# Another order for the same work: a planner that shakes its due times by a stored list of seeds

## The chip, the cores and the metric

The kernel runs on one core of one Trainium2 chip. Five engines matter here: TensorE (PE), VectorE (DVE), ScalarE (ACT), GpSimd (POOL) and SyncE (SP). Each runs its own instructions in the order in which they stand in the program, and waits on semaphores for the others. SP and POOL issue nearly all the DMA transfers of this kernel. The metric is device microseconds (us), the median over runs; lower is better.

## The reference

The input `x` has two batches of 1024 rows by 2048. Each batch goes through a quantized product with its own context matrix and then through a feed-forward product with one shared matrix of ternary weights. Both are added to the row they came from, with a gate:

```python
def fake_quant(x, scale, zp):
    q = jnp.clip(jnp.round(x / s + z), 0.0, 255.0)
    return (q - z) * s
...
# feed-forward
s = 127.0 / jnp.clip(jnp.max(jnp.abs(x), axis=-1, keepdims=True), 1e-05, None)
xq = jnp.clip(jnp.round(x * s), -128.0, 127.0) / s
scale_w = 1.0 / jnp.clip(jnp.mean(jnp.abs(weight)), 1e-5, None)
tw = jnp.clip(jnp.round(weight * scale_w), -1.0, 1.0)
out = jnp.einsum('bsi,oi->bso', xq, tw) / scale_w
...
x = x + jnp.tanh(g_xattn[0]) * matmul(fake_quant(layernorm(x)), fake_quant(ctx))
x = x + jnp.tanh(g_ffn[0]) * feed_forward(layernorm(x), weight)
```

## The kernel before

A batch is eight row tiles of 128 rows; tiles 0 to 7 are batch 0, tiles 8 to 15 are batch 1, and the two share eight places in `resid`. The kernel has these kinds of work, each of them written as a function that hands steps to a planner:

- `norm1` takes the statistics of a row tile (four instructions of 512 columns on DVE, then the aggregate), the root on ACT, a chain of small DVE instructions, the quantizer on ACT, eight transposes on PE (`turn_steps`), and two copies of the transposed tile from PSUM into the arena, each on ACT or on DVE.
- `context` loads 1 MB of the context (a chunk: 256 rows by 1024 columns, so eight chunks for each half `h`), rounds it on ACT (L612) and clips it on DVE (L616).
- `first` is the product of one row tile with one half of the context: eight units of four matmuls (L641), one for each chunk, and one addition to the residual on DVE (L647).
- `norm2`, `weight_load`, `weight_sum`, `weight_scale` and `weight_turn` prepare the second stage. The weights come in twice for nine of the sixteen row tiles: once for the mean of their magnitudes, once to be quantized, turned on PE (L1054) and clipped (L1062, L1064).
- `couple` and `plain` are the second product for batch 0 (matmuls at L778 and L824). For batch 1, `differences` and `bring_back` make sums and differences of weight blocks and `seven` does the product with seven block products where eight would be usual (L949).
- `evict2` adds a finished product to the residual (L762), `store` writes it out (L769).

Three product buffers (`mm`) and two transpose buffers (`tr`) fill the PSUM. The arena in SBUF has 32 slots, for which contexts, weights and turned tiles compete.

The order of all this is not written by hand. Every step has its engine or engines, a modelled duration, a due time, and what it reads, writes, takes and gives back. `Order.run` plays the steps forward once in modelled time. At each turn it takes, over all engines, the step that can start first, and among those that tie to 1e-6 us the one that is due first. `work_back` plays the result backward and gives each step the latest time at which it could have started; these times are the due times of the next run. `give_out(12)` does twelve such rounds, keeps the run with the smallest modelled end, and then calls the steps in that order. Where a step may go to ACT or DVE, `run` sends it to the one that would end it sooner.

The planner's times are only a model. The real order on each engine is what it gives out; the real times come from semaphores. Four loads stand outside of it: the entry function issues the row tiles 0 (in two halves), 1 and 2 itself, before the branch, always in the order of L1997 (issued at L1998). In the plan they are steps on a made-up engine `PRE` that issues nothing (L462).

Of the kernel before, what the change touches and what calls it, by code (L numbers as in the profile page):

```python
# [108 lines left out]
class Order:  # L109
# [5 lines left out]
    START = {"PRE": 0.5}  # L115
    BRANCH = 4.6

# [35 lines left out]
    @staticmethod  # L153
    def room(pool, k, reserve=0, prefer=None):

        ends = sorted(t for t, _ in pool)
        at = ends[k + reserve - 1]
        if k == 2:
            at = max(at, min(max(pool[i][0], pool[i + 1][0]) for i in range(0, len(pool) - 1, 2)))
        return at  # L160

    @staticmethod
    def pick(pool, at, k, reserve=0, prefer=None):
        if k == 2:
            for i in prefer or range(0, len(pool) - 1, 2):
                if max(pool[i][0], pool[i + 1][0]) <= at + 1e-9:
                    return [i, i + 1]
        if prefer is None:
            return [min(range(len(pool)), key=lambda i: (pool[i][0], i))]
        for i in prefer:  # L170
            if pool[i][0] <= at + 1e-9:
                return [i]

    def run(self, due):
        steps, N = self.steps, len(self.steps)
        waits = [len(s[3]) for s in steps]
        early = [s[7] for s in steps]
        pools = {k: [(0.0, -1)] * n for k, n in self.sizes.items()}
        left = dict(self.users)
        till = {}  # L180
        free, open_ = {}, {}
        dma_free, dma_last = 0.0, -1
        begin, end, where, slots = [0.0] * N, [0.0] * N, [None] * N, [None] * N
        pred = [[] for _ in steps]
        links = self.links = [{} for _ in steps]
        last = {}
        order = []

        def put(n):
            for e, w in steps[n][0]:  # L190
                open_.setdefault(e, {})[n] = w

        for n in range(N):
            if not waits[n]:
                put(n)
        for _ in range(N):
            best = None
            for e, cand in open_.items():
                fe = free.get(e, self.START.get(e, self.BRANCH))
                for n, w in cand.items():  # L200
                    at = early[n]
                    if at < fe:
                        at = fe
                    if best is not None and at > best[0] + 1e-6:
                        continue
                    take = steps[n][4]
                    if take:
                        at = max(at, self.room(pools[take[0]], *take[1:]))
                        if at == float("inf"):
                            continue  # L210
                    if len(steps[n][0]) > 1:
                        key = (at, due[n], n, at + w, e)
                    else:
                        key = (at, due[n], n, 0.0, e)
                    if best is None or at < best[0] - 1e-6 or key[1:] < best[1:]:
                        best = key
            if best is None:
                self.stuck = [n for c in open_.values() for n in c], order, slots
                return None
            at, _, n, _, e = best  # L220
            ways, _, _, _, take, give, dma, _ = steps[n]
            if len(ways) > 1:
                ends = []
                for e2, w2 in ways:
                    ends.append((max(at, free.get(e2, self.BRANCH)) + w2, e2, w2))
                fin, e, w = min(ends)
                at = fin - w
            else:
                w = ways[0][1]
            for e2, _ in ways:  # L230
                del open_[e2][n]
            if take:
                pool = pools[take[0]]
                idx = slots[n] = self.pick(pool, at, *take[1:])
                for i in idx:
                    if pool[i][1] >= 0:
                        pred[n].append(pool[i][1])
                        links[n][pool[i][1]] = True
                    pool[i] = (float("inf"), -1)
            if e in last:  # L240
                pred[n].append(last[e])
            last[e] = n
            begin[n] = at
            where[n] = e
            fin = at + w
            free[e] = fin
            if dma:
                if dma_last >= 0:
                    pred[n].append(~dma_last)
                dma_free = max(dma_free, fin) + abs(dma)  # L250
                dma_last = n
                fin = dma_free + self.LANDING
            end[n] = fin
            order.append(n)
            for m, i in give:
                for j in range(steps[m][4][1]) if i is None else (i,):
                    left[m, j] -= 1
                    t = till.get((m, j))
                    if t is None or fin + self.LAG > t[0]:
                        t = (fin + self.LAG, n)  # L260
                    till[m, j] = t
                    if not left[m, j]:
                        pools[steps[m][4][0]][slots[m][j]] = t
            for m in self.follow[n]:
                same = len(steps[m][0]) == 1 and steps[m][0][0][0] == e and not dma
                t = fin + (0.0 if same else self.LAG)
                if t > early[m]:
                    early[m] = t
                waits[m] -= 1
                if not waits[m]:  # L270
                    put(m)
        return order, begin, end, where, slots, pred
# [45 lines left out]

    def give_out(self, runs=12, tell=None):
        self.prepare()  # L320
        due = [s[1] for s in self.steps]
        best = None
        for r in range(runs):
            res = self.run(due)
            if res is None:
                if tell:
                    tell("stuck")
                break
            if tell:
                tell(f"run {r}: {max(res[2]):.2f}")  # L330
            if best is None or max(res[2]) < max(best[2]):
                best = res
            back = self.work_back(res)
            due = back
        assert best is not None, "the steps that are left wait for each other's buffers"
        self.best = best
        order, begin, end, where, slots, pred = best
        for n in order:
# [6 lines left out]
def centred(  # L345
# [198 lines left out]
    def norm1(tiles, due, pieces=1):  # L544
# [33 lines left out]
        for i, t in enumerate(tiles):  # L578
# [12 lines left out]
            for g in range(pieces):  # L591
                m = step(
                    "ACT", 0.3 + 1.85 / pieces, due, (lambda f, g: lambda slots=None: f(g, slots))(quant, g),
                    rd=[key("sc")] + xk(t), wr=[k2("q", g)], take=None if g else ("q8", 1),
                )
                by = by if g else m
# [32 lines left out]
    def first(t, h, due):  # L629
# [22 lines left out]
        for c in range(C):  # L652
            give = [cx[b, h, c]["by"]]
            if c == C - 1:
                give.append(turned["aT", t, "by"])
            n = step(
                "PE", 0.865, due, (lambda c: lambda slots=None: mult(c, slots))(c),
                rd=[("aT", t, 2 * c // C), ("ca", b, h, c)], wr=[("pm", t)],
# [5 lines left out]
    def norm2(tiles, due):  # L664
# [4 lines left out]
        def mean(i, t):  # L669
            if i == 0:  # L670
                s["nm"], s["vm"] = tiny(n), tiny(2 * n)
# [113 lines left out]

    def couple(ta, tb, q, due, pieces, last):

        s = {}
        by = None
        for n, (o0, o1) in enumerate(pieces):  # L790
            for i, t in enumerate((ta, tb)):
# [5 lines left out]

                w = 16 * (0.027 + 0.0472 * (o1 - o0))
                end = last and n == len(pieces) - 1
                m = step(  # L800
# [9 lines left out]

    def plain(t, h, due, last):
        s = {}
        by = None
        for i in range(2):
# [14 lines left out]
            for c0 in (0, 4):  # L829
                end = last and i == 1 and c0 == 4  # L830
                m = step(
                    "PE", 1.73, due, (lambda f, c0: lambda slots=None: f(c0, slots))(mult, c0),
                    rd=q_keys(t, q, 0, 4), wr=[("pl", t, h)], take=None if (i or c0) else ("mm", 1),
# [66 lines left out]
    def seven(ta, tb, due, final=False):  # L900
# [39 lines left out]
        for k, (name, bank, left, right, need, new, dest) in enumerate(products):  # L940
# [19 lines left out]
            for i, (cs, ns) in enumerate(parts):  # L960
                give = []
                if i == len(parts) - 1:
# [6 lines left out]
                m = step(  # L969
                    "PE", 3.46 / len(parts), due + 3.46 * (k + i / len(parts)),  # L970
                    (lambda f, cs, ns: lambda slots=None: f(cs, ns, slots))(mult, cs, ns),
# [165 lines left out]
    for q in range(NQ):  # L1137
        for ta in (0, 2):
            pieces = [(o, o + 1) for o in range(4)] if q == 0 else [(0, 4)]
            couple(ta, ta + 1, q, due, pieces, q == NQ - 1)  # L1140
            due += 6.9
    for t in range(4, MT):
        for h in range(2):
            plain(t, h, due, h == 1)
            due += 6.9
# [23 lines left out]

    plan.give_out(12)  # L1170

# [867 lines left out]
```

## Time and profile before

| | |
|---|---|
| median of 3 runs | 484.92 us (484.38 to 485.58) |
| the profiled execution | 485.77 us |
| its span, first to last instruction | 484.0 us |
| PE busy | 454.3 us |
| DVE busy | 340.6 us |
| ACT busy | 258.4 us |
| DMA, mean over the span | 211 GB/s |
| first transposes on PE | 12.72 us |
| first product on PE | 21.23 us |

The profile lists instructions by line, engine and operation. A "wait" names the engine and line that came last before an idle engine went on. The granted clock of PE was 0.996 in the mean. Matmuls overlap in the records, so the sum of their durations is larger than the busy time. Up to about 95 us the DMA queues move around 400 GB/s (rows, contexts and weights of batch 0).

### The profile page before, as it was taken

The page shows a single profiled execution, that of the slowest core. Times are in us where ns is not written, and L with a number is a line of the kernel's source. Part 1 is how long each engine was busy: PE and PEld are TensorE (multiplying, and loading weights), DVE is VectorE, ACT ScalarE, POOL GpSimd, SP SyncE. Part 2 cuts the span into 40 slices and gives each one's busy share as a digit, 9 for nine tenths or more (in the row PEclk, how much of TensorE's full clock was granted, in tenths as well). Part 3 has the DMA queues.
Part 4 walks back from the last instruction along what each step waited for, and adds up shares of the span by engine and source line. Part 5 has one row for each costly group of instructions (what it writes and reads, how often), then busy time and mean ns, then how long its engine had stood idle before and what let it go on. Part 6 is the DMA issues. An engine that isn't in the chain of part 4 may idle for free.

```text
span 484.0 us, 6296 instructions
## 1 busy us (share of the span) xinstructions
PE 454.3 (94%) x2564; PEld 225.0 (46%) x2564; DVE 340.6 (70%) x534; ACT 258.4 (53%) x200; POOL 21.2 (4%) x39
## 2 busy tenths in 40 slices
PE   0499999999999999999998999999999999999994
PEld 0244444444588545444444444444444454444442
DVE  4988899928789987798975997124776987333342
ACT  3886699867989998711129663002656770000000
POOL 0000000000031101111101000000000000000000
PEclk9999999999999999999999999999999999999998
DMA  8999999791099986899979411062000012131304
GB/s 318 405 415 413 413 419 389 267 357 78 1 362 393 332 293 185 244 387 393 398 318 335 187 45 43 1 244 105 0 0 1 1 43 108 68 130 45 130 22 158
DMA packets 21857, 102.20 MB, mean 211 GB/s; under 512 B 1980, under 2 KB 1980, under 8 KB 16700
## 3 DMA queue, kind: packets, MB, share of 16 engines
q1 hardware_dynamic: 15008, 67.11, 35.0%
q0 software_dynamic: 6800, 34.61, 20.0%
q8 instruction: 22, 0.36, 0.3%
q14 instruction: 15, 0.12, 0.1%
q10 hardware_dynamic: 12, 0.00, 0.0%
HBM read 80.74 MB, written 20.97 MB: 210 GB/s over the span
## 4 chain that ended last, share of the span: by engine, by line
PE 71%; DMA 11%; ACT 7%; DVE 5%; issue 4%; DVEq 0%; ACTq 0%; POOL 0%; POOLq 0%
PE mm L641 42%; PE mm L949 20%; DMA arena<-in_ctx_dram 9%; PE mm L778 6%; ACT bytes L1047 3%; PE tr L513 3%; ACT bytes L586 2%; DMA out_dram<-resid 2%; DVE arena L521 1%; DVE arena L1064 1%; ACT arena L612 1%; DVE resid L762 1%; DMA row<-in_L_xattn_x_zp_dram 1%; DVE resid L647 1%; DVE strip L685 0%
## 5 line engine op out<-in xcount | busy, mean ns | idle before, releaser
L641 PE MATMUL mm<-arena 128*128 128x512 f16 x1024 | 226.2, 380 | 3.1 <-ACT arena L521 1.9
L641 PEld LDWEIGHTS <-arena 128*128 128x128 f16 x1024 | 99.2, 98 | 119.8 <-ACT arena L521 2.0
L949 PE MATMUL mm<-arena 128*128 128x512 fp8e4 x448 | 97.5, 379 | 0.0
L762 DVE SCALAR_TENSOR_TENSOR resid<-mm,am,resid 128x1024 f32<-128x1024 f32 (+1 forms) x53 | 58.0, 1099 | 55.6 <-PE mm L949 44.6
L612 ACT ACTIVATE arena<-arena,scal 128x2048 int16<-128x2048 f32 x32 | 62.8, 1994 | 42.7 <-DMA arena<-in_ctx_dram 42.7
L647 DVE SCALAR_TENSOR_TENSOR resid<-mm,scal,resid 128x1024 f32<-128x1024 f32 x32 | 40.8, 1281 | 42.9 <-PE mm L641 31.6
L949 PEld LDWEIGHTS <-arena 128*128 128x128 f16 x448 | 43.7, 98 | 51.9
L778 PE MATMUL mm<-arena 128*128 128x128 fp8e4 (+1 forms) x448 | 58.2, 288 | 0.9 <-DVE resid L762 0.9
L824 PE MATMUL mm<-arena 128*128 128x512 fp8e4 x256 | 55.6, 379 | 0.0
L679 ACT ACTIVATE arena<-resid,strip 128x2048 f32<-128x2048 f32 x16 | 32.0, 2000 | 40.7 <-DVE strip L673 40.6
L685 DVE TENSOR_REDUCE strip<-arena 128x1 f32<-128x2048 f32 x16 | 36.5, 2279 | 11.8 <-ACT arena L679 11.8
L521 ACT CAST arena<-tr 128x1024 f16<-128x1024 int8 x37 | 36.1, 1009 | 14.4 <-PE tr L513 12.4
L778 PEld LDWEIGHTS <-arena 128*128 128x128 f16 x448 | 33.2, 98 | 22.5 <-issue 1.0
L550 DVE BATCH_NORM_STATS2 stats<-resid 128x6 f32<-128x512 f32 x64 | 39.8, 674 | 0.8 <-DVE off_centre L2002 0.8
L824 PEld LDWEIGHTS <-arena 128*128 128x128 f16 x256 | 25.0, 98 | 30.0
L586 ACT ACTIVATE bytes<-resid,strip 128x2048 int8<-128x2048 f32 (+1 forms) x17 | 33.2, 1985 | 10.5 <-DVE strip L569 10.5
L521 DVE CAST arena<-tr 128x1024 f16<-128x1024 int8 x27 | 32.7, 1217 | 5.2 <-PE tr L513 4.3
L861 DVE TENSOR_TENSOR arena<-arena 128x2048 fp8e4<-128x2048 fp8e4 x16 | 35.9, 2275 | 0.0
L735 ACT ACTIVATE bytes<-resid,strip 128x2048 int8<-128x2048 f32 x16 | 33.0, 2087 | 3.8 <-DVE strip L708 3.8
L1047 ACT ACTIVATE bytes<-arena,scal 128x2048 int8<-128x2048 f32 x16 | 31.4, 2000 | 0.0
L513 PE MATMUL tr<-ident,bytes 128*128 128x128 f16 x256 | 20.0, 224 | 11.5 <-ACT bytes L586 9.6
L1064 DVE TENSOR_SCALAR arena<-tr 128x1024 fp8e4<-128x1024 int8 x23 | 27.1, 1216 | 3.4 <-PE tr L1054 2.4
(61 smaller groups left out, 185.7 us busy)
## 6 DMA issues: line engine op xcount, KB each, us to landing
arena<-in_ctx_dram SPq DMA_DIRECT2D x16, 1024.0 KB, 13.7
arena<-in_L_ffn_weight_dram SPq DMA_DIRECT2D x16, 1024.0 KB, 8.3
arena<-in_ctx_dram POOLq DMA_DIRECT2D x16, 1024.0 KB, 8.7
out_dram<-resid SPq DMA_DIRECT2D x31, 512.0 KB, 7.0
arena<-in_L_ffn_weight_dram POOLq DMA_DIRECT2D x9, 1024.0 KB, 8.8
resid<-in_x_dram POOLq DMA_DIRECT2D x8, 1024.0 KB, 12.6
resid<-in_x_dram SPq DMA_DIRECT2D x7, 1024.0 KB, 16.0
awayT<-arena SPq DMA_DIRECT2D x8, 512.0 KB, 4.5
```

What stands on the lines that cost most here:

```text
L521: (nc.scalar.copy if engine == "ACT" else nc.vector.tensor_copy)(d[:, ts(h, n)], v[:, ts(h, n)])
L550: nc.vector.bn_stats(stats6[:, t % 4, c, :], res(t)[:, ts(c, 512)])
L586: nc.scalar.activation(q["q"][:, ts(g, w)], res(t)[:, ts(g, w)], AF.Identity, bias=s["bi"][:, i : i + 1], scale=s["sc"][:, i : i + 1],)
L612: nc.scalar.activation(slot16(slots[0]).bitcast(I16), s["w"], AF.Identity, scale=rs2)
L641: nc.tensor.matmul(pm[t][:, ts(q, U)], a[:, c, j, :], o[:, j, ts(q, U)], start=(c + j == 0), stop=(c + j == C),)
L647: nc.vector.scalar_tensor_tensor(v, pm[t], g1, v, ALU.mult, ALU.add, accum_out=acc[:, i : i + 1])
L685: nc.vector.tensor_reduce(s["vm"][:, n + i : n + i + 1], s["dev", t], AX.X, ALU.max)
L762: lambda: nc.vector.scalar_tensor_tensor(v, ps(), am2[:, t : t + 1], v, ALU.mult, ALU.add),
L778: nc.tensor.matmul(ps[:, o0 * P : o1 * P], a[:, c, j, :], w[:, j, o0:o1], start=(c + j == 0), stop=(c + j == C),)
L824: nc.tensor.matmul(s["pm"][:, ts(i, U)], a[:, c, j, :], w[:, j, :], start=(c + j == 0), stop=(c + j == C),)
L949: nc.tensor.matmul(s[bank][:, ts(n, U)], a[:, c, j, :], v[:, c, j], start=new and c + j == 0, stop=c + j == 4, skip_group_check=not new,)
L1047: nc.scalar.activation(s["q"], wl[ot]["w"], AF.Identity, scale=sw)
```

## The change

The planner gets new rules for its choice, and its result is shaken.

- `run` looks at all open steps. Among those that can start no later than 0.3 us (`WIN`) after the earliest, it takes the one that is due first.
- A step with two engines goes where it would end first, after a `lean` of its own is added to its second engine.
- `settle` does the twelve rounds as before. After that, `give_out` goes through 95 stored seeds. Each of them shifts the due times (and the leans) of the steps around one moment by random amounts; the shifts add up. Then `run` plays the steps once with the shaken times, and that order is used.
- The modelled start after the branch moves from 4.6 to 5.4 us, and some modelled PE durations go down by about 1%.
- `couple` and `plain` give back the slot of a turned tile after all of their pieces, where only those of the last columns did so; `norm1` and `norm2` no longer assume which tile of a pair comes first.

No step is added or taken away, and each step does what it did.

```diff
-    BRANCH = 4.6
+    BRANCH = 5.4
+    WIN = 0.3
+    LEAN = 0.0
...
-    def run(self, due):
+    def run(self, due, lean):
...
+            open_ += ready
+            rooms, ways = {}, {}
+            for n in open_:
+                at, take = early[n], steps[n][4]
+                if take:
+                    kind = take[0], take[1], take[2] if len(take) > 2 else 0
+                    if kind not in rooms:
+                        rooms[kind] = self.room(pools[kind[0]], *kind[1:])
+                    at = max(at, rooms[kind])
+                best = None
+                for i, (e, w) in enumerate(steps[n][0]):
+                    s = max(at, free.get(e, self.START.get(e, self.BRANCH)))
+                    f = s + w + (lean[n] if i else 0.0)
+                    if best is None or f < best[0]:
+                        best = f, s, e, w
+                ways[n] = best
+            first = min(b[1] for b in ways.values())
...
+            n = min((due[n], n) for n in open_ if ways[n][1] <= first + self.WIN)[1]
...
+    def shake(self, due, lean, begin, seed):
+        r = random.Random(seed)
+        span = max(begin)
+        mid, half = r.uniform(0.0, span), r.choice((4.0, 12.0, 40.0, span))
+        share, by = r.choice((0.1, 0.3, 1.0)), r.choice((2.0, 6.0, 15.0))
+        due, lean = list(due), list(lean)
+        for n, t in enumerate(begin):
+            if abs(t - mid) <= half and r.random() < share:
+                due[n] += r.gauss(0.0, by)
+                if len(self.steps[n][0]) > 1:
+                    lean[n] += r.gauss(0.0, 0.8)
+        return due, lean
...
+    def give_out(self, seeds=()):
         self.prepare()
...
+        res, due, lean = self.settle()
+        begin = res[1]
+        for seed in seeds:
+            due, lean = self.shake(due, lean, begin, seed)
+        if seeds:
+            res = self.run(due, lean)
...
-                "PE", 0.865, due, (lambda c: lambda slots=None: mult(c, slots))(c),
+                "PE", 0.855, due, (lambda c: lambda slots=None: mult(c, slots))(c),
...
-                end = last and n == len(pieces) - 1
+                end = n == len(pieces) - 1
...
-    plan.give_out(12)
+    plan.give_out((
+        596853, 876363, 279267, 840775, 26681, 303858, 939078, 813524, 764831, 209546, 902833, 961729,
...
+    ))
```

## The prediction

> **What bounds the kernel now.** I read the page's busy shares first, then the slices, then who TensorE (PE) waited for, then the opening in order of time.
>
> ```profile
> span 484.0 us, 6296 instructions
> PE 454.3 (94%) x2564; PEld 225.0 (46%) x2564; DVE 340.6 (70%) x534; ACT 258.4 (53%) x200; POOL 21.2 (4%) x39
> PE   0499999999999999999998999999999999999994
> ```
>
> PE is the bound: 454.3 of 484.0, and its row of slices is full but for the two at the front and the last. The time to be had or lost is PE's idle time, 29.7 us. The view of PE's waits says where it lies:
>
> ```profile
> PE tr L513 <- ACT bytes L586: 9.6, 2, 5.2
> PE tr L444 <- ACT row L2003: 7.7, 1, 7.7
> PE mm L641 <- ACT arena L521: 1.9, 1, 1.9
> PE tr L513 <- DVE arena L521: 1.3, 1, 1.3
> PE mm L778 <- DVE resid L762: 0.9, 1, 0.9
> PE mm L641 <- DVE arena L616: 0.8, 2, 0.6
> ```
>
> 9.6 + 7.7 + 1.3 = 18.6 us are the opening, before PE's first product. The other waits, with three under 0.7 us (0.6, 0.5, 0.3), are 1.9 + 0.9 + 0.8 + 1.4 = 5.0 us in all. The remaining 6.2 us are the tail behind PE's last matmul (477.8 to 484.0). So a new order can win at most 5.0 us behind the opening, unless it shortens the opening or the tail. The opening, in order of time (start, duration, engine):
>
> ```profile
> 5.74 0.69 DVE L550 BATCH_NORM_STATS2 stats<-resid 128x6 f32<-128x512 f32 x1 [0.78 <-DVE off_centre L2002]
> 6.35 1.86 DVE L550 BATCH_NORM_STATS2 stats<-resid 128x6 f32<-128x512 f32 x3
> 8.25 0.26 DVE L555 BATCH_NORM_AGGREGATE strip<-stats 128x2 f32<-128x24 f32 x1
> 8.59 1.28 ACT L559 ACT_TABLE_LOAD   x1 [0.93 <-DVE strip L555]
> ...
> 11.43 2.37 ACT L586 ACTIVATE bytes<-resid,strip 128x1024 int8<-128x1024 f32 x2 [1.25 <-DVE strip L569]
> 12.72 0.61 PE L513 MATMUL tr<-ident,bytes 128*128 128x128 f16 x4 [4.42 <-ACT bytes L586]
> ...
> 20.40 1.03 PE L513 MATMUL tr<-ident,bytes 128*128 128x128 f16 x8 [5.17 <-ACT bytes L586]
> 21.23 3.68 PE L641 MATMUL mm<-arena 128*128 128x512 f16 x12
> ...
> 26.68 3.63 PE L641 MATMUL mm<-arena 128*128 128x512 f16 x16 [0.46 <-DVE arena L521]
> ```
>
> Four statistics of row tile 0, its mean and variance, the root on ScalarE (ACT), the quantizer, the transposes: one serial chain that nothing hides. From 21.23 on PE hardly stops. The loads that the chain stands on (issues, and time to landing):
>
> ```profile
> L1998 SPq DMA_DIRECT2D resid<-in_x_dram x4: 327/360/415, 0.7 to 4.8; - x4
> DMA to landing us min/median/max: 4.1/5.0/6.6
> ```
>
> The first half of tile 0 lands at 0.75 + 4.1 = 4.9, the second (issued 1.24) at 1.24 + 5.0 = 6.2, tile 2 (issued 4.8) at 4.8 + 6.6 = 11.4. Tile 1, as large as tile 2, stands between the last two; half way, 8.8, is my estimate for it.
>
> **The change, part by part.** No instruction is added or taken away on PE: 477 planned steps in both orders, so PE's own work is worth 0. Four clips or copies go over from VectorE (DVE) to ACT; both have idle time, worth 0 on the path as long as neither is what PE waits for. The lower weights (0.855 for 0.865 and so on), the window and the leanings cost nothing themselves; they only choose the order. So I walk the new order, with durations from the rows of before.
>
> *Opening.* In the planner's own list the load of row tile 1 now stands ahead of the second half of tile 0. But these four loads are not issued by the planner: the entry function issues them in a fixed order, tile 0's second half first. On DVE the new order is: two statistics of tile 0, one of tile 1, the two of the scales (L447, L448), and only then the last two of tile 0. Queued behind the statistic that waits for tile 1 are therefore the whole chain above, and ACT and PE behind it. DVE: two statistics to 7.0; tile 1 lands at 8.8, statistic to 9.5; the scales 0.24; two statistics 1.24 to 11.0; so the aggregate starts at 11.05 instead of 8.25, **+2.8**. Bounds: landing at 6.2 would leave 0.7 + 0.24 = +0.9, landing at 11.4 +5.4. I take 8.8, by sizes.
>
> The quantizer starts at 14.25, its halves end at 16.6. ACT's new order: copy of the first transposes 16.65 to 17.65, root of tile 1 to 18.0, two context chunks (1.9 each, where now one stands there) to 21.85, root of tile 2, which waits for DVE's aggregate at 21.95, to 22.3, then tile 1's quantizer, 2.05, to 24.35. PE's order still has tile 1's transposes ahead of the first product, so they start at 24.4 instead of 20.40: **+4.0**, my term for the opening.
>
> *What PE regains to 75 us.* Then the first products find more chunks ready. T1, T2 stand for eight transposes (0.45 us), a unit is four matmuls at 71.66 / 332 = 0.2158 us each (the chain's long stretch), 0.863 us. New order: two units, T2 (its quantizer ends at 26.4), then units for tiles 1, 2 and 0, whose last inputs, DVE's copies at 27.8 and 29.0 and clip at 29.7, come before PE is there. I followed the queues to the transposes of tile 7: every input came ahead of PE, the narrowest by under 1 us (tile 2's second copy, 40.9). The three waits of this stretch now (0.5, 0.2, 0.6) are saved, 1.3. Loads in this stretch come at the rate of the DMA queues (412 GB/s in 21 to 45 us); the SP order differs in the first two chunks alone, worth 0.
>
> Weighed against a rule: the first 12 matmuls took 3.52 us up to the next transposes, 0.29 each, and 16 later ones 0.227 each, while the window around them shows a granted clock of 1.00. The Trainium skill, "TensorE: Matmul & The Clock Gate", Part 1, says that the array runs at half rate until about 3.4 us of sustained work and falls back after an idle window of that length. By it the longer wait (18.3 to 24.4 here) speaks against the change; but the present gap of 5.17 us is over the limit too, so by the rule and by the row the slow start is paid once in each order: 0. If only the new gap paid, up to 1.7 us (estimate from that page) would be added.
>
> *Feed-forward weights, 118 to 205 us.* The waits of 0.9, 0.6 and 0.3 here come from two transpose buffers and three product buffers. The new order puts the sum of the weights behind 104 product units instead of 113 and ends the weight turns later (24 couples and 6 plain pieces ahead of the last one, now 23 and 0), so ACT and DVE have more time per turn: saved 1.8. My walk finds one new wait, at weight tile 6, where both transpose buffers are full until DVE has clipped tile 5: 0.7.
>
> *Turn to batch 1.* Now:
>
> ```profile
> 259.20 2.00 ACT L612 ACTIVATE arena<-arena,scal 128x2048 int16<-128x2048 f32 x1 [0.45 <-DMA arena<-in_ctx_dram]
> 261.11 2.08 ACT L586 ACTIVATE bytes<-resid,strip 128x2048 int8<-128x2048 f32 x1
> 264.14 2.12 PE L641 MATMUL mm<-arena 128*128 128x512 f16 x9 [1.85 <-ACT arena L521]
> ```
>
> A chunk that came late holds ACT, and ACT holds the copy that PE wants: 1.85 us. In the new order three plain pieces (5.2 us) stand between the transposes of tiles 8 and 9 and the first product. Tile 0's last store is now some 14 us of PE work nearer to this place, and POOL loads tile 8 after it: store 7.0, load 12.6 to landing, still ahead of need. Saved 1.85.
>
> *Rest.* From 264 to the last matmul PE idles 0.1 now; the new interleaving of banks can only lose. Bounds: 0, and 5.0, as much as the present order loses. I take 0.8, what PE now loses to late clips (L616). The tail has the same last piece (half a bank, one store of 256 KB) behind a store issued 0.4 us before PE ends, as now: 0, still 6.2.
>
> **Sum.** +4.0 opening, -5.0 (1.3 + 1.8 + 1.9) waits gone, +0.7 + 0.8 new: +0.5. The profiled execution took 485.77 with its span of 484.0 (1.77 around it); that is 0.85 above the median, 484.92, to which I apply the difference: **485.4 us**. A difference below 0.3% (1.45 us) counts as no change, about what a measurement can tell.
>
> **Rivals.**
>
> 1. *The late opening stays* (slower). DVE, ACT and PE are all shifted by the same wait for tile 1, so waits between them return as they were: +4.0, 488.9. For it: in 21 to 45 us DVE is busy 20.2 of 24 us and ACT 19.2, so neither catches up quickly. Against: the chunks loaded meanwhile. It decides once new waits pass 2.5 us.
>
> 2. *Tile 1 lands early, or no new wait comes* (faster). At a landing of 6.2 the aggregate is 0.95 late instead of 2.8: 485.4 - 1.85 = 483.5. Without new waits 485.4 - 1.5 = 483.9, with both 482.0; I price the case at 483.2. Against: tiles 1 and 2 share the 5.2 us between the landings at 6.2 and 11.4, 2.6 us per MB, the 405 GB/s that the page has for the second slice.
>
> 3. *The order hardly changes*: ruled out, PE's sixth step already differs.
>
> **How the numbers follow.** Forecast 0.40, rival 1 0.38, rival 2 0.22. Range: from 483.2 less 0.5 for my reading of the opening, 482.7, to 488.9 plus 0.9 for one more wait like that at L778, 489.8. Faster 0.22, same 0.40, slower 0.38.
>
> **What would show it.** In the changed profile (lines stand 8 earlier): DVE's third statistic starts near 8.8 behind a wait for a load; first transposes near 15.5, tile 1's near 24.4; no wait over 1 us at the first product of batch 1; a tail of 6.2. I am wrong if the third statistic starts by 7.5, if PE waits over 2.5 us in all behind 25 us, or if a store or a load of batch 1 holds it near 260.

## The result, and the profile after

The changed kernel took 488.67 us (median of four runs, 488.02 to 489.27) where the kernel before took 484.73 beside it (four runs, 484.38 to 485.58). The ratio is 1.0079, with a 95% interval of 1.0060 to 1.0097: slower by 0.8%, or 3.9 us. The forecast of 485.4 was 3.3 us too low; the range of 482.7 to 489.8 holds the result. The prediction had given "same" a chance of 0.40 and "slower" 0.38.

The profiled execution took 488.58 us, 2.8 more than that of before (485.77); its span is 486.8, also 2.8 more. The profiled run of before lay 1.0 above its own median and that of after 0.1 below, which is the rest of the 3.9. All sums below are in spans and have to explain 2.8.

The head of the page, the kernel after:

```profile
span 486.8 us, 6291 instructions
PE 455.7 (94%) x2564; PEld 225.8 (46%) x2564; DVE 337.3 (69%) x530; ACT 262.7 (54%) x203; POOL 21.2 (4%) x39
PE   0199999999998999989999999999999999999995
PEclk9999999999999999998999999999999999999999
```

PE has the same 2564 matmuls and transposes, yet is busy 1.4 us longer. Behind the opening its row of slices (12.2 us each) has an 8 in the slices from 146 and from 207 us, and the row of the granted clock has its 8 next to the second, from 219 us on. PE's waits, the kernel after (engine, line, what came last; us in total, times, longest):

```profile
PE tr L505 <- ACT bytes L578: 13.0, 2, 7.4
PE tr L436 <- ACT row L2004: 7.5, 1, 7.5
PE mm L770 <- DVE resid L754: 2.0, 1, 2.0
PE tr L505 <- ACT arena L513: 1.4, 1, 1.4
PE tr L505 <- DVE arena L1056: 1.2, 2, 1.0
```

The opening is 13.0 + 7.5 + 1.4 = 21.9 where it was 18.6: **+3.3**. The other waits are 2.0 + 1.2 = 3.2 where they were 5.0: **-1.8**. All waits of before behind the opening are gone, the batch turn's 1.85 among them; two new places, at 153 to 158 us and at 216 us, took 3.2 back. With **+1.4** of busy time and a tail of 6.0 for 6.2 (**-0.2**) the sum is +2.7, the 2.8 up to rounding.

The opening in order of time, the kernel after (start, duration, engine):

```profile
5.48 1.29 DVE L542 BATCH_NORM_STATS2 stats<-resid 128x6 f32<-128x512 f32 x2
8.94 0.69 DVE L542 BATCH_NORM_STATS2 stats<-resid 128x6 f32<-128x512 f32 x1 [2.18 <-DMA resid<-in_x_dram]
9.55 0.14 DVE L439 COPY scal<-tr 128x4 f32<-128x4 f32 x1
9.69 1.27 DVE L542 BATCH_NORM_STATS2 stats<-resid 128x6 f32<-128x512 f32 x2
10.99 0.26 DVE L547 BATCH_NORM_AGGREGATE strip<-stats 128x2 f32<-128x24 f32 x1
...
15.47 0.61 PE L505 MATMUL tr<-ident,bytes 128*128 128x128 f16 x4 [7.44 <-ACT bytes L578]
...
23.65 1.03 PE L505 MATMUL tr<-ident,bytes 128*128 128x128 f16 x8 [5.57 <-ACT bytes L578]
24.48 3.26 PE L633 MATMUL mm<-arena 128*128 128x512 f16 x8
```

The third statistic is row tile 1's, and it waits 2.18 us for that load. Everything behind it in DVE's queue, the last two statistics of tile 0 above all, is 2.74 us later than before (aggregate 10.99 for 8.25), and so are the quantizer and the first transposes.

Now a stretch that the prediction's walk left out. In order of time, the kernel after, 207 to 226 us:

```profile
207.19 7.07 PE L770 MATMUL mm<-arena 128*128 128x512 fp8e4 x32
214.09 1.89 PE L816 MATMUL mm<-arena 128*128 128x512 fp8e4 x8
214.30 0.75 DVE L754 SCALAR_TENSOR_TENSOR resid<-mm,am,resid 128x512 f32<-128x512 f32 x1 [4.13 <-PE mm L770]
214.97 2.28 DVE L853 TENSOR_TENSOR arena<-arena 128x2048 fp8e4<-128x2048 fp8e4 x1
217.16 0.74 DVE L754 SCALAR_TENSOR_TENSOR resid<-mm,am,resid 128x512 f32<-128x512 f32 x1
217.96 8.32 PE L770 MATMUL mm<-arena 128*128 128x512 fp8e4 x30 [1.98 <-DVE resid L754]
```

PE makes the two products of a couple (32 matmuls) and eight matmuls of a plain piece; then it wants a free product buffer. The couple's two additions free it. DVE idles 4.13 us until the products are ready, does the first addition, then a weight difference of 2.28 us (L853) that stands between the two in its queue, and only then the second. PE waits 1.98 us, and what follows costs as much again. Windows over the same stretch (window, us, busy us of PE, PEld, DVE, ACT and POOL with their counts, granted clock, DMA share, GB/s), the kernel after:

```profile
205.00:216.00 11.00, 10.98 (x51) 4.90 (x50) 6.87 (x6) 5.27 (x4) 0.71 (x1) 1.00 0.51 144
218.40:221.80 3.40, 3.40 (x10) 1.19 (x9) 3.40 (x2) 0.00 (x0) 1.80 (x3) 0.50 0.85 270
221.80:230.00 8.20, 8.20 (x39) 3.72 (x38) 3.75 (x4) 0.94 (x1) 0.70 (x1) 1.00 0.99 380
```

For 3.41 us PE's granted clock is 0.50: 10 matmuls in a stretch that holds some 16 at the rate of the line below (39 in 8.20). Half of 3.41 is 1.7 us, and that is PE's longer busy time, but for -0.3 that I can't place.

### The profile page after: what moved, and what is told of

Read it like the earlier page. It is cut to its first block, busy times and chain, and to the rows that moved or that the text cites. A ratio compares the mean times of both kernels' runs of the same rounds, so it can differ in the third digit from the quotient of the medians.

```text
span 486.8 us, 6291 instructions
## 1 busy us (share of the span) xinstructions
PE 455.7 (94%) x2564; PEld 225.8 (46%) x2564; DVE 337.3 (69%) x530; ACT 262.7 (54%) x203; POOL 21.2 (4%) x39
## 4 chain that ended last, share of the span: by engine, by line
PE 90%; ACT 3%; DVE 2%; issue 1%
PE mm L633 45%; PE mm L941 20%; PE mm L816 11%; PE mm L770 10%; PE tr L505 3%; PE tr L1046 1%; DVE arena L1056 1%; ACT bytes L578 1%; ACT bytes L1039 1%; ACT arena L604 1%; ACT arena L513 1%; DVE arena L853 0%; DVE resid L754 0%; DVE arena L513 0%; ACT arena L1054 0%
## 5 line engine op out<-in xcount | busy, mean ns | idle before, releaser
L770 PE MATMUL mm<-arena 128*128 128x128 fp8e4 (+1 forms) x448 | 60.2, 292 | 2.0 <-DVE resid L754 2.0
L513 ACT CAST arena<-tr 128x1024 f16<-128x1024 int8 x41 | 39.9, 1012 | 25.5 <-PE tr L505 20.4
L853 DVE TENSOR_TENSOR arena<-arena 128x2048 fp8e4<-128x2048 fp8e4 x16 | 36.1, 2280 | 0.0
L513 DVE CAST arena<-tr 128x1024 f16<-128x1024 int8 x23 | 27.7, 1217 | 7.0 <-PE tr L505 6.9
L1056 DVE TENSOR_SCALAR arena<-tr 128x1024 fp8e4<-128x1024 int8 x22 | 26.0, 1218 | 7.1 <-ACT arena L1054 5.4
```

What stands on the lines that cost most here:

```text
L513: (nc.scalar.copy if engine == "ACT" else nc.vector.tensor_copy)(d[:, ts(h, n)], v[:, ts(h, n)])
L770: nc.tensor.matmul(ps[:, o0 * P : o1 * P], a[:, c, j, :], w[:, j, o0:o1], start=(c + j == 0), stop=(c + j == C),)
```

## The experiments

Theory, after the comparison: the loss has two separate parts, each one step given out at a bad place. (A) Tile 1's statistic and the scales ahead of tile 0's last statistics, some 2.5 to 3 us. (B) One weight difference between two additions at 214 us, 2 us of waiting and 1.7 us of half clock. The rival: the new order shifts everything, these two are only where it shows, and with either mended the loss turns up elsewhere. Seven of the kernels move one, two or three steps after the plan is made; nothing else changes. Step 20 is the first statistic of row tile 1, steps 5 to 8 are the four of tile 0, step 1 the scales, steps 11 and 12 small DVE steps of tile 0 behind the aggregate; 516 and 517 are the two products of the couple at 207 us, 518 and 520 their additions, 935 the weight difference.

**Tile 1's statistic behind tile 0's four**

```
         self.best = order, begin, end, where, slots, pred = res
+        order = list(order)
+        order.remove(20)
+        order.insert(order.index(8) + 1, 20)
```

> The changed kernel with one step moved: on VectorE the first statistic of row tile 1 stands behind the four of tile 0, not ahead of the last two. Theory A (the opening's wait for tile 1 is paid at the end): the wait of 2.2 us at the third statistic goes, first transposes near 12.5 instead of 15.5, those of tile 1 near 21 instead of 23.7, and 488.7 falls by 2 to 3 us to about 486. Rival (context chunks come too late anyway, the wait is hidden): PE idles later for what it gains, and the time stays within 0.7 us of 488.7. The wait of 2.0 us near 216 us and the slow clock after it stay under both.

487.65 us, ratio to the kernel before 1.0057 (1.0038 to 1.0076): 1 us won, not 2 to 3. A miss, and the opening of this kernel shows why:

```profile
8.09 0.16 DVE L442 COPY scal<-tr 128x4 f32<-128x4 f32 x1 [1.30 <-PE tr L439]
8.24 1.86 DVE L545 BATCH_NORM_STATS2 stats<-resid 128x6 f32<-128x512 f32 x3
10.02 0.24 DVE L550 BATCH_NORM_AGGREGATE strip<-stats 128x2 f32<-128x24 f32 x1
14.48 0.61 PE L508 MATMUL tr<-ident,bytes 128*128 128x128 f16 x4 [6.43 <-ACT bytes L581]
```

The scales (L442, L443) still stood ahead of tile 0's last two statistics. They need a small product of PE that is ready only at 8.09. Behind tile 1's load that had cost nothing; with that load out of the way it became the wait, 1.30 us, and one statistic of tile 1 still runs ahead of the aggregate. One wait had hidden another.

**The second addition ahead of the weight difference**

```
         self.best = order, begin, end, where, slots, pred = res
+        order = list(order)
+        order.remove(520)
+        order.insert(order.index(935), 520)
```

> The changed kernel with one step moved: on VectorE the residual addition of row tile 1 (last columns of batch 0's couple) stands ahead of the difference T2/0 that now holds it for 2.3 us. Theory B (the wait near 216 us is this queue, and the half clock from 218.4 to 221.8 follows from the wait): both go, 2.0 + 1.7 us, so about 485.0. Rival 1 (the clock falls on its own account): the wait goes, the half clock stays, about 486.7. Rival 2 (PE waits for something else behind it, such as weights or a buffer): no change, 488.7.

484.99 us, ratio 1.0001 (0.9989 to 1.0013), span 483.0: 3.8 us less than the kernel after. The same place, now with both additions together:

```profile
214.12 1.89 PE L819 MATMUL mm<-arena 128*128 128x512 fp8e4 x8
214.32 1.41 DVE L757 SCALAR_TENSOR_TENSOR resid<-mm,am,resid 128x512 f32<-128x512 f32 x2 [4.13 <-PE mm L773]
215.85 7.07 PE L773 MATMUL mm<-arena 128*128 128x512 fp8e4 x32
```

and its window:

```profile
218.40:221.80 3.40, 3.40 (x17) 1.56 (x16) 3.40 (x2) 0.00 (x0) 1.79 (x3) 1.00 0.55 166
```

PE no longer waits, the clock stays at 1.00 and the same window holds 17 matmuls for 10. PE is busy 453.8 us, 1.9 less than in the kernel after. One step moved by one place in DVE's queue takes both the 2.0 and the half clock away. That is part B, and shown.

**Both of these moves**

```
+        order.remove(20)
+        order.insert(order.index(8) + 1, 20)
+        order.remove(520)
+        order.insert(order.index(935), 520)
```

> The changed kernel with both moves of the two runs before. Theory A and B together, if the two are independent: 2.7 + 3.7 us less, about 482.3, which is faster than the kernel before (484.7). If the opening is hidden: 485.0; if the clock falls anyway: 484.0.

484.03 us, ratio 0.9979 (0.9967 to 0.9991). Short of the expectation by 1.7 us, as the first move was by itself: this run had the same half mended opening.

**The kernel before, with tile 1's statistic moved to where the new order has it**

```
         order, begin, end, where, slots, pred = best
+        order = list(order)
+        order.remove(20)
+        order.insert(order.index(7), 20)
```

> The kernel before with the opening's fault alone: on VectorE the first statistic of row tile 1 stands ahead of the last two of tile 0. Theory A: it waits for the load till about 8.9, the chain starts 2.8 us later, less the 0.6 us that this statistic would take later, and nothing behind makes it up: 484.7 + 2 to 3 = 487.2. Rival (the opening has slack, the loss comes from elsewhere): within 0.7 us of 484.7.

488.90 us, ratio 1.0077 (1.0056 to 1.0098), span 486.9, +2.9 against before; I had expected +2 to +3 on the time, and by medians it was more. This one step alone makes the old order as slow as the new one. Its opening:

```profile
8.93 1.88 DVE L553 BATCH_NORM_STATS2 stats<-resid 128x6 f32<-128x512 f32 x3 [2.12 <-DMA resid<-in_x_dram]
23.01 1.04 PE L516 MATMUL tr<-ident,bytes 128*128 128x128 f16 x8 [5.17 <-ACT bytes L589]
23.84 4.85 PE L644 MATMUL mm<-arena 128*128 128x512 f16 x12
```

Tile 1's transposes start 2.6 later (23.01 for 20.40), the first twelve matmuls take 1.2 longer (4.85 for 3.68), and the batch turn's wait shrinks from 1.85 to 1.02: +2.6 + 1.2 - 0.8 = +3.0. The old order's other waits are all still there. Here rival 1's mechanism, everything shifted together, is seen at work.

**The new order with the opening as before**

```
         self.best = order, begin, end, where, slots, pred = res
+        order = list(order)
+        order.remove(1)
+        order.insert(order.index(11) + 1, 1)
+        order.remove(20)
+        order.insert(order.index(12) + 1, 20)
```

> The changed kernel with VectorE's whole opening as in the kernel before: the four statistics of tile 0, their aggregate, then the scales, then the chain, and tile 1 behind it. The run with one step moved still had the scales ahead of tile 0's last statistics, and these wait till about 8.0 us for PE's small product. Theory A: first transposes near 12.5, those of tile 1 near 20.9 (23.7 in the changed kernel), the time 488.7 less 2 to 2.8, about 486.2; the wait near 215 us and a half clock behind it stay. Rival (late context chunks hide the opening): 488 or more.

486.44 us, ratio 1.0024 (1.0009 to 1.0039), as expected. Its opening:

```profile
8.04 0.26 DVE L552 BATCH_NORM_AGGREGATE strip<-stats 128x2 f32<-128x24 f32 x1
12.52 0.61 PE L510 MATMUL tr<-ident,bytes 128*128 128x128 f16 x4 [4.43 <-ACT bytes L583]
21.20 1.04 PE L510 MATMUL tr<-ident,bytes 128*128 128x128 f16 x8 [6.07 <-ACT bytes L583]
```

The opening is back to within 0.8 us at tile 1's transposes, and the wait of 1.97 us with its half clock is still there. Part A is worth 2.2 us by the medians (488.67 to 486.44) and by the spans (486.8 to 484.6), 2.7 by the ratios (0.0055 of 484.7), and it doesn't touch part B.

**Both places mended**

This is the last edit with the two lines on step 520 from above behind it.

> That opening together with the residual addition of row tile 1 ahead of the difference T2/0 near 216 us. Theory: the two add up, 485.0 (the second alone) less 2 to 2.8, about 482.6, 0.5% faster than the kernel before. Rival (late chunks hide the opening): 484 to 485.

482.43 us, ratio 0.9940 (0.9920 to 0.9960), span 480.6: faster than both kernels, by 0.6% than before and by 1.4% than after. PE's waits in this kernel:

```profile
PE tr L512 <- ACT bytes L585: 10.5, 2, 6.1
PE tr L443 <- ACT row L2011: 7.5, 1, 7.5
PE tr L512 <- ACT arena L520: 1.4, 1, 1.4
PE tr L512 <- DVE arena L1063: 1.2, 2, 1.0
```

Behind the opening only the 1.2 that stood at 153 to 158 us is left. The two parts add up: by the medians 3.7 and 2.2 alone, 6.2 together; by the ratios 3.8 and 2.7 alone, 6.7 together (1.0079 less 0.9940). The rival, that the loss would turn up elsewhere, is out.

**Why the plan gave out these orders.** Four more kernels look for the belief of the planner that was wrong.

*Without the seeds.* The 95 numbers are left out, so that the new rules and the twelve rounds alone set the order:

```
-    plan.give_out((
-        596853, 876363, 279267, 840775, 26681, 303858, 939078, 813524, 764831, 209546, 902833, 961729,
...
-    ))
+    plan.give_out(())
```

> The changed planner with an empty list of seeds: its rules alone. In its order VectorE's very first instruction is tile 1's statistic, ahead of all four of tile 0. Theory: the wrong order of the opening comes from the new rules and not from the shaking, so that this kernel starts still later: all four statistics begin near 9.6 instead of two of them at 9.7, first transposes near 16.7, and the time is 489 to 491. Rival (the shaking by the seeds is what costs): no more than 486.

493.13 us, ratio 1.0156 (1.0130 to 1.0183), above both expectations. The late opening is there without any seed:

```profile
8.94 0.69 DVE L542 BATCH_NORM_STATS2 stats<-resid 128x6 f32<-128x512 f32 x1 [3.69 <-DMA resid<-in_x_dram]
```

and PE has waits behind it that the kernel after doesn't have:

```profile
PE mm L633 <- DVE arena L608: 2.8, 1, 2.8
PE mm L633 <- DVE arena L513: 1.8, 1, 1.8
PE tr L1046 <- DVE arena L1056: 1.4, 1, 1.4
```

The wait of 2.8 us also brought a stretch of half clock, the one of 1.8 did not. So the perturbation gains 0.8% over the bare rules (1.0156 less 1.0079). The late opening is there before any shaking; whether the new rules or the model's new times bring it, no run separates.

*The entry loads in the plan's order.* The plan has tile 1's load ahead of tile 0's second half; here the program does the same:

```
-        for t, lo, hi in ((0, 0, K // 2), (0, K // 2, K), (1, 0, K), (2, 0, K)):
+        for t, lo, hi in ((0, 0, K // 2), (1, 0, K), (0, K // 2, K), (2, 0, K)):
```

> The changed kernel with the four first loads issued in the order that its plan believed: tile 0's first half, tile 1, tile 0's second half, tile 2. Theory: the statistic of tile 1 no longer waits long (load near 7.5), but tile 0's second half now lands near 8.8 and holds the last two: the aggregate moves from 11.0 to about 10.1 and the time falls by 0.5 to 1 us, about 488. Rival (only the disagreement of plan and loads costs, the order itself is good): back to the opening of before, 486.

488.51 us, ratio 1.0069 (1.0042 to 1.0096). From its opening:

```profile
7.55 0.69 DVE L542 BATCH_NORM_STATS2 stats<-resid 128x6 f32<-128x512 f32 x1 [0.96 <-DMA resid<-in_x_dram]
9.09 0.16 DVE L439 COPY scal<-tr 128x4 f32<-128x4 f32 x1 [0.84 <-PE tr L436]
9.24 1.27 DVE L542 BATCH_NORM_STATS2 stats<-resid 128x6 f32<-128x512 f32 x2
15.02 0.61 PE L505 MATMUL tr<-ident,bytes 128*128 128x128 f16 x4 [5.97 <-ACT bytes L578]
```

Tile 1's statistic comes 1.4 earlier (7.55 for 8.94), the transposes only 0.45 (15.02 for 15.47). The expected size came out, but the wait in between is another: the scales wait 0.84 us for PE's small product, which itself starts 1 us later here (8.46 for 7.46), and tile 0's last two statistics follow at once; no wait for tile 0's second half shows. In time no difference from the kernel after can be told, so that plan and program agree on the loads is not enough. With the program's load order and DVE's old opening (486.44 us, first transposes at 12.52) the new order does better; the plan should have known that order.

*The second product given out behind the first one's addition.* This asks whether the planner's view of a product buffer differs from the program's. In the plan each of the two products of a couple has a key of its own, and the first addition may start when its own product ends, about 3.5 us ahead of the second. The trace above has that addition at 214.30, after both.

```
+        order.remove(517)
+        order.insert(order.index(518) + 1, 517)
```

> The changed kernel with the second product of the couple near 210 us given out after the first product's residual addition. In the plan the addition of row tile 0 may start when its own product is done; in the changed kernel it started only when both were (214.30, PE ended both at 214.09). Theory: the two products share one buffer and the wait covers what stands ahead in the order, so the addition now starts near 210.8, the difference behind it too, and row tile 1's addition is no longer held; the price is that PE waits about 1 us for the addition between the two products. The wait of 2.0 us becomes 1.0, and with no wait near 2 us the half clock does not come: 488.7 - 1.0 - 1.7 = 486.0. Rival (the half clock comes with any wait here, or on its own): 487.7. Rival (the addition was held by something else, not by the second product): it still starts near 214, and the time is 488.7 or more.

486.09 us, ratio 1.0013 (0.9999 to 1.0027). The place in this kernel:

```profile
211.58 0.75 DVE L757 SCALAR_TENSOR_TENSOR resid<-mm,am,resid 128x512 f32<-128x512 f32 x1 [0.68 <-PE mm L773]
212.39 3.61 PE L773 MATMUL mm<-arena 128*128 128x512 fp8e4 x16 [0.84 <-DVE resid L757]
```

The addition starts 2.7 us earlier (211.58), although the couple itself begins 0.7 later, and now PE waits 0.84 us for it: with the products given out one after the other, the addition waits for one alone, and with both ahead of it, for both. The whole buffer carries the dependence, not its half. The 2-us wait and the half clock are gone. So the difference between the two additions was harmless in the plan's time, and stood in the way in the program's.

*The planner told that the entry loads have a fixed order*, with the same 95 seeds:

```
+        due = [s[1] - 1e4 if s[0][0][0] == "PRE" else t for t, s in zip(due, self.steps)]
         if seeds:
```

> The changed planner told the true order of the four first loads, with the same 95 seeds; the whole plan comes out different. Its VectorE order has two statistics of tile 0, the scales, the other two, and one of tile 1 ahead of the aggregate; the difference T2/0 still stands ahead of row tile 1's addition. Theory: the opening is that of the run with one step moved (aggregate near 10, first transposes near 14.5) and the wait near 215 us may come again: 486 to 489. Rival (knowing the loads is all that the plan lacked): below 484.

488.33 us, ratio 1.0053 (1.0034 to 1.0071). The aggregate starts at 10.00 and the wait at 214.5 of 1.98 us is there again; PE's second long wait of the opening now stands right ahead of the first product (4.1):

```profile
PE mm L634 <- DVE arena L609: 4.7, 2, 4.1
PE mm L771 <- DVE resid L755: 2.0, 1, 2.0
```

A corrected model with the old seeds gives another order, and not a clearly better one (1.0053 beside 1.0079, with intervals that overlap). Whether seeds looked for anew, with a model that knows both the load order and the whole buffers, would beat 482.43 wasn't tried.

## Why the prediction was right or wrong

- *The opening, +4.0.* Right in mechanism, 0.7 too high. Tile 1's statistic started at 8.94 (8.8 forecast), the aggregate at 10.99 (11.05), the first transposes at 15.47 (15.5). The 0.7 lies behind that: tile 1's at 23.65 (24.4), because tile 2's aggregate, for which the walk had ACT wait until 21.95, started at 20.94 and didn't hold ACT, which began tile 1's quantizer at 21.52 (22.3). By the spans of the experiments the opening is worth 2.2 to 2.9 us.
- *Waits gone, -5.0.* Right in each of its three parts: no wait of PE from the first product to 153 us, none of the old weight stage, none at the batch turn.
- *One new wait, +0.7, where both transpose buffers are full.* Right in kind (L1056, the clip of a weight tile), 1.2 in two waits.
- *The step that failed is the count of new waits: "My walk finds one new wait, at weight tile 6 ... 0.7", and "Rest. From 264 to the last matmul ... I take 0.8".* The first covered 118 to 205 us, the batch turn 259 to 264, the rest what follows. From 205 to 259 us the sum had no term, and there the wait of 2.0 us came, with 1.7 us of half clock behind it: 3.7, for the 0.8 of a rest that turned out to be 0. The three steps on DVE could have been read off the new order; that PE would have to wait for them needed one thing more, that the first addition starts only when both products are done.
- *The clock, priced at 0.* In the window behind the new wait the granted clock was 0.50 for 3.41 us. For the opening's slow start the forecast weighed the Trainium skill, "TensorE: Matmul & The Clock Gate", Part 1, by which an idle window of about 3.4 us drops the clock. The forecast's estimate from that page, 1.7 us, is the price measured; the page's length of the gap is not, since 1.98 us was enough here. So a new wait in mid-kernel should have had nearly its own length again as an upper bound.
- *The sum.* Against +0.5: opening -0.7, the wait foreseen +0.5, the rest -0.8, the wait not foreseen +2.0, busy time +1.4, tail -0.2, together +2.2, and with that +2.7 in spans. The other 1.0 of the 3.3 us by which the forecast fell short is no part of the change's working: of the two profiled executions that of before lay 0.85 above the median given, that of after 0.1 below its own.
- *Rival 1* had nearly the time (488.9) and its condition, new waits over 2.5 us, came true with 3.2; this was also one of the signs by which the prediction said it would be wrong. Its mechanism did not: the old waits didn't return; a new one and the half clock took their place. So it is partly luck that the range, whose upper end is this rival's time and 0.9 more, holds the result. In the old order with the late statistic the mechanism did hold.
- *Rival 2* needed an early landing of tile 1; it came at 8.9. Its price, and the bound of +0.9 for the aggregate, took the scales at 0.24 us, without the wait for PE's small product that the run with one step moved showed (until 8.09); with it even an early landing would have left about +1.3 (8.24 and two statistics, 1.30, instead of 8.25; an estimate). Its other half, no new wait, is nearly what the kernel with both places mended has (1.2 us is left): with the opening mended too, it gives 482.43.

Left open: the kernel before ran between 483.75 and 486.96 in the runs beside these experiments, and nothing in the profiles says why; differences under 1 us between two medians here carry no weight.

## What to carry to other kernels

A planned order is as good as the plan's belief of what each instruction waits for. Compare that belief with the trace at two kinds of place before trusting any search on top of it: work issued outside the plan (here loads in another order), and buffers that the plan splits finer than the program's waits do. On an in-order queue one such error costs everything queued behind it, so in a diff of two orders, look for a long instruction that has come to stand between the parts of what another engine waits for, and price its wait with the clock it may cost.

## What the runs showed of the hardware

- PE's granted clock fell to 0.50 for 3.41 us in every profile with a PE wait of 1.97 to 2.75 us behind the opening's first products (six kernels, five of them at the same place), within 0.6 us of PE's resuming. It didn't fall after waits of 1.85 us (the batch turn before), 1.78, 1.02 and 0.84. The Trainium skill, "TensorE: Matmul & The Clock Gate", Part 1, gives about 3.4 us of idleness for this; these runs show that about 2 us can do. It doesn't do so in every execution: one of the twelve runs of the new order with the opening as before took 484.28 us with a mean granted clock of 0.999, where 3.41 us at 0.50 alone would make it 0.996 (the others: 0.994 to 0.997, median 486.44). That run has no trace, so its wait isn't known.
- One reading fits these traces: the falls lie whole multiples of 3.41 us after the clock's first rise (191.15 us in five of them). On a raster of that length, each of the six waits lay inside one cell and took 0.58 to 0.81 of it; the wait of 1.85 us lay inside one cell, too, but took 0.54 of it, and those of 1.78 and 1.02 lay across an edge. So the idle share of a cell may decide, but no run varied the place of a wait against the raster; that is only argued.
- The slow start after the opening isn't of one length. Twelve first matmuls took 3.68 us in the kernel before and 4.85 in the same kernel with its opening 2.6 later, so that the delay of 2.6 us had grown to 3.8 behind them. The window view gives a granted clock of 1.00 there, but the traces' first record of the full clock comes only 2.7 us after the start of tile 1's transposes in the first of these kernels and 5.0 us in the second (3.6 in the kernel after); ahead of it they hold no record.
